# Layer 0 of a four-layer state-space kernel: one shared projection for two scan directions, and two convolution taps per hop instead of three

## The chip, the cores and the metric

The kernel runs on one core of one Trainium2 chip, all in float32. The metric is the time of one execution in microseconds (us), as the device reports it. The core's engines are called by the profile's names: PE (matrix products; PEld is its weight load), DVE (the vector engine), ACT (the scalar engine with its function tables), POOL (GpSimd) and SP, which only issues transfers (SPq, and ACTq for those that ACT issues).

## The reference

Four layers, each with a residual, work on an image batch `x` of shape 2 x 96 x 96 x 96. Each of them runs a selective state-space scan over sequences in four directions. Only layer 0 is changed. Cut to what matters, it is

```python
xin, z = split(in_proj(group_norm(x)))            # 192 channels each
t = gelu(batch_norm(conv3x3(xin, off1_w) + off1_b))
offset = tanh(conv1x1(t, off2_w)) * small         # two numbers per pixel
x_s = bilinear_sample(xin, grid + offset)
xt = x_s cut into 6x6 windows                     # L = 36
xs4 = [rows, columns, rows reversed, columns reversed]
x_dbl = einsum('bkdl,kcd->bkcl', xs4, x_proj_weight)   # k = 4 directions
dts, Bs, Cs = x_dbl[:6], x_dbl[6:22], x_dbl[22:38]
delta = softplus(dt_projs_weight @ dts + bias)
h[l] = h[l-1] * exp(delta[l] * A) + delta[l] * x[l] * B[l];  y[l] = h[l] . C[l]
out = x + out_proj(layer_norm(sum of the four y) * silu(z))
```

Directions 0 and 2 read the same sequence (rows), forwards and backwards; directions 1 and 3 read the columns. So `x_proj_weight` of 0 and 2 is applied to the same numbers, and that of 1 and 3 too.

## The kernel before

**Machine and hops.** A `Machine` object plays one scan over a list of jobs (`Machine.scan`, L449). A job is one direction over one piece of sequence; it has eight steps, called hops, one for each pair of a quarter of the 16 states and a half of the 192 channels. All engines' instructions are written out hop by hop in Python and are kept in that order on each engine. Every buffer is a ring, so an engine that is late holds up the others when their rings are full. Layer 0 has its own machine with T = 288 columns (E = 0); layers 1 to 3 (the trunk) share one with T = 384 (E = 1).

**What a hop issues, in order.** `four_C` (a transfer that spreads four rows of C over 128 partitions) and `four_B` (one matrix product with the 0/1 matrix `sel` that spreads four rows of B, written `pb<-p,sel`), both only in every second hop; transfers that spread delta and delta*x; `sum_states` of two hops earlier (three products `py<-hC,zs`); `decay` of the next hop (three ACT exponentials `dA<-d`); then what was put off to the `slot` of this hop: copies and activations on ACT whose inputs PE made in the hop before; then DVE's four instructions (two products `pd<-w,pb`, two scans `hs<-dA,pd`); `finish` of an earlier job (DVE, reads `py`); the preambles of coming jobs; the background generators (`hop`, L612); and POOL's `hC<-hs,C`. The rings of `hs` and `hC` hold three hops, `dA` two for each sense of direction, `pb` two.

**Layer 0's jobs.** The image is cut into 32 strips of six rows. A strip is eight jobs, 64 hops: two pairs of directions, (0, 2) on rows and (1, 3) on columns, each over two half strips of 288 columns, two directions each. The second job of each two `joins` the first one: both sum into the same `py`. This document writes "hop 7.3" for hop 3 of job 7 of a strip (both counted from 0).

**Preamble** (L362), ten hops ahead of its job (`lead` = 10): in the hop whose number in the eight is 7, two products `pm<-xr,w_wx` (or `xc`) give 80 rows: 6 for dt, 16 for B from row 32, 16 for C from row 64. In the next slot ACT copies them to `j.p` and issues the transfer of the C rows to memory. Then two products `pm<-p,w_dtw` (hops 0 and 1), two ACT evictions `v<-pm,w_scol` (slots 1 and 2), the softplus in slot 2 between two loads of function tables, the transfer of delta, and POOL's `du<-v,xr`. PE has one bank, `pm`, for all of this; `banks = (7, 0, 1)` keeps those hops for the preamble, and the background work takes `pm` in hops 2 to 6 (`bank`, L310).

**Background work of a strip.** `samples` (L824) makes the next strip: affine of the input, then the offsets' convolution (the loop over `tap`), four groups (`po<-x,w_offs`) of nine products of 96 x 96 x 288, each into the one bank `po`; three taps to a hop, then the eviction `t<-po` on ACT in the next slot; then the GELU (with two table loads), the 1x1 convolution `pm<-t,w_off` with tanh, the halving, seven bilinear steps on POOL, the input projection `pm<-top,w_in` and two copies of each piece. `ending` (L735) finishes the last strip: mean and variance (`pm<-yn,mats`, `pm<-sq,mats`), the affine, the gate z (`pm<-xn,w_in`, SiLU), the output projection (`pm<-yn,w_out`). Both run side by side and take turns at `pm`.

## Time and profile before

| | us |
|---|---|
| median of 3 runs | 25900.6 (25885.88 to 25911.11) |
| the profiled execution | 26051.65, its span 26049.9 |
| layer 0, first scan to end of the last (in the profile) | 136.4 to 6863.7 |
| trunk, first scan to last | 7191.5 to 26024.5 |

The time outside the span is 1.75 us. A hop with nothing late lasts 2.92 us, which is DVE's own four instructions. The table below has the mean time of each job of a strip, from the start of its first scan to that of the next job's, over strips 2 to 30 of the profiled execution; it is read from the timeline, two scans to a hop. "Other DVE work" is what DVE does besides its four instructions a hop; "idle" is DVE's.

| job | time | other DVE work | idle | where the idle time lies |
|---|---|---|---|---|
| 0 | 34.06 | 2.78 | 7.95 | hop 1: 3.60, hop 2: 0.49, hop 3: 1.43, hop 4: 1.48, hop 6: 0.95 |
| 1 | 24.90 | 0 | 1.41 | hop 3: 1.22 |
| 2 | 25.09 | 0.98 | 0.73 | hop 3: 0.58 |
| 3 | 27.27 | 0 | 3.67 | hop 2: 1.06, hop 3: 2.40 |
| 4 | 25.54 | 0.98 | 1.20 | hop 1: 0.36, hop 3: 0.72 |
| 5 | 25.06 | 1.76 | 0.08 | |
| 6 | 24.50 | 1.30 | 0 | |
| 7 | 24.64 | 0 | 1.12 | hop 3: 0.59, hop 7: 0.53 |
| strip | 211.05 | 7.8 | 16.1 | |

The convolution's stretch, hop 7.3 to the start of hop 1.0, takes 49.9 us in the mean, and between 41.6 and 65.1 us; whole strips take 201.0 to 228.0 us. The granted PE clock is either full or half in this record, and changes at multiples of 3.41 us.

### The profile page before, as it was taken

Reading aid. Unit: us, or ns where it says so; the run is one execution under the profiler, and the core shown is the slowest. Engines: PE = TensorE matmul, PEld = TensorE weight load, DVE = VectorE, ACT = ScalarE, POOL = GpSimd, SP = SyncE. Lnnn points to the kernel's source line nnn. Section 1 sums busy time; section 2 is a strip of 40 time slices with the busy share of each in tenths; the row PEclk is TensorE's granted clock in tenths of the full one; section 3 lists DMA queues with packets and bytes.
Section 4 is the critical chain, followed back from the end, with each engine's and each line's share of the span. In section 5 each row is a group of like instructions: output and inputs, shape, how many; then the busy total and the mean of one; then the engine's idle time right before and its main releaser. Section 6 shows DMA issues by size and latency. Waiting matters only on the chain.

```text
span 26049.9 us, 281866 instructions
## 1 busy us (share of the span) xinstructions
PE 20979.3 (81%) x70044; PEld 6516.9 (25%) x70044; DVE 24561.8 (94%) x28451; ACT 18515.7 (71%) x40207; POOL 18448.3 (71%) x9188
## 2 busy tenths in 40 slices
PE   7888888888677788888887887778877887877778
PEld 2222222222222222222222222222222222211112
DVE  7989999999589999988999999999999999999999
ACT  5666666666678777777777776677766777666666
POOL 6777777777477777766776666676667766776677
PEclk6655655655577777788877765557755677655566
DMA  3333333333455555555555554555555555544444
GB/s 106 112 107 111 114 110 111 113 112 110 86 150 149 151 158 174 154 149 154 167 172 152 160 154 147 156 166 163 151 153 163 160 161 153 154 148 146 145 145 147
DMA packets 3307209, 3707.97 MB, mean 142 GB/s; under 512 B 781136, under 2 KB 3284822, under 8 KB 3305464
## 3 DMA queue, kind: packets, MB, share of 16 engines
q1 hardware_dynamic: 2587480, 3207.89, 41.0%
q10 hardware_dynamic: 718080, 482.05, 7.7%
q8 instruction: 552, 9.04, 0.1%
q14 instruction: 1097, 8.99, 0.1%
HBM read 2933.11 MB, written 755.57 MB: 142 GB/s over the span
## 4 chain that ended last, share of the span: by engine, by line
DVE 29%; ACT 11%; issue 11%; PE 8%; DMA 3%; POOL 1%; SPq 1%; ACTq 0%; DVEq 0%; POOLq 0%
DVE hs L157 18%; DVE pd L157 10%; PE pm L157 5%; ACT dA L157 5%; ACT L157 2%; PE py L157 2%; SPq L157 1%; PE pb L157 1%; ACT v L157 1%; DVE y L157 1%; POOL hC L157 1%; DMA C<-p 1%; ACT big L157 1%; DMA z<-sz 0%; ACTq L157 0%
## 5 line engine op out<-in xcount | busy, mean ns | idle before, releaser
L157 POOL TENSOR_TENSOR hC<-hs,C 128x1152 f32<-128x1152 f32 (+1 forms) x6656 | 15592.1, 2344 | 7016.7 <-DVE hs L157 4681.1
L157 DVE TENSOR_TENSOR_SCAN hs<-dA,pd 128x772 f32<-128x772 f32 (+2 forms) x13312 | 16047.1, 1245 | 383.7 <-ACT dA L157 241.0
L157 ACT ACTIVATE dA<-d,w_alog 128x384 f32<-128x384 f32 (+1 forms) x19968 | 10281.2, 579 | 4028.9 <-DVE hs L157 3798.1
L157 PE MATMUL py<-hC,zs 128*32 128x384 f32 (+1 forms) x39936 | 7749.6, 676 | 2177.2 <-POOL hC L157 1867.4
L157 DVE TENSOR_TENSOR pd<-w,pb 128x772 f32<-128x772 f32 (+2 forms) x13312 | 8746.4, 701 | 528.3 <-PE pb L157 212.1
L157 PE MATMUL pb<-p,sel 16*128 16x386 f32 (+1 forms) x6656 | 4173.0, 719 | 486.1 <-ACT turn L157 199.1
L157 ACT ACT_TABLE_LOAD x2466 | 3163.9, 1283 | 138.5 <-ACT v L157 92.4
L157 PEld LDWEIGHTS py<-hC,zs 128*32 128x32 f32 x39936 | 1233.4, 129 | 7302.6 <-POOL hC L157 4329.6
L157 PE MATMUL pm<-p,w_dtw 6*96 6x384 f32 (+1 forms) x3328 | 2112.9, 729 | 1106.8 <-ACT v L157 583.2
L157 PEld LDWEIGHTS pb<-p,sel 16*128 16x128 f32 x6656 | 1369.3, 255 | 2528.9 <-DVE hs L157 859.5
L157 PE MATMUL pm<-x,w_taps 96*96 96x384 f32 x3456 | 1591.5, 607 | 192.9 <-ACT v L157 121.7
L157 PE MATMUL pm<-x,w_in 128*96 128x384 f32 (+1 forms) x2448 | 1282.7, 675 | 166.3 <-ACT v L157 75.1
L157 PE MATMUL pm<-xs,w_wx 96*80 96x384 f32 x2304 | 1360.5, 734 | 68.2 <-ACT xs L157 41.1
L157 ACT COPY w<-hc 128x6 f32<-128x6 f32 x4416 | 861.9, 195 | 750.8 <-DVE pd L157 368.9
L157 PEld LDWEIGHTS pm<-p,w_dtw 6*96 6x96 f32 x3328 | 559.8, 219 | 2640.0 <-ACT v L157 1309.0
L157 ACT ACTIVATE v<-pm,w_scol 96x384 f32<-96x384 f32 (+1 forms) x1664 | 909.0, 546 | 214.0 <-issue 100.5
L157 POOL TENSOR_TENSOR du<-v,xs 96x768 f32<-96x768 f32 x576 | 1043.8, 1812 | 7.7 <-ACT v L157 7.6
L157 PE MATMUL po<-x,w_offs 96*96 96x288 f32 x2304 | 885.5, 536 | 49.0 <-ACT x L157 43.0
L157 PEld LDWEIGHTS pm<-x,w_taps 96*96 96x96 f32 x3456 | 632.9, 199 | 1135.7 <-issue 730.9
L157 ACT COPY hc<-hs 128x3 f32<-128x3 f32 x4608 | 827.4, 180 | 4.3 <-DVE hs L157 4.3
L157 PE MATMUL py<-xs,diag 96*96 96x384 f32 x1152 | 654.4, 658 | 151.9 <-ACT y L157 151.9
L157 PEld LDWEIGHTS pm<-x,w_in 128*96 128x96 f32 (+1 forms) x2448 | 503.1, 225 | 980.3 <-issue 448.1
(225 smaller groups left out, 12276.6 us busy)
## 6 DMA issues: line engine op xcount, KB each, us to landing
d<-delta SPq DMA_DIRECT2D x3456, 192.0 KB, 3.7
w<-du SPq DMA_DIRECT2D x3456, 192.0 KB, 3.3
C<-C SPq DMA_DIRECT2D x2304, 192.0 KB, 3.6
d<-delta SPq DMA_DIRECT2D x1536, 144.0 KB, 2.6
w<-du SPq DMA_DIRECT2D x1536, 144.0 KB, 2.6
delta<-v ACTq DMA_DIRECT2D x576, 288.0 KB, 2.6
du<-du SPq DMA_DIRECT2D x576, 288.0 KB, 4.1
C<-C SPq DMA_DIRECT2D x1024, 144.0 KB, 2.8
```

Source lines behind the costliest of these rows:

```text
L157: r = traced(*args, **kwargs)
```

## The change

1. **One projection for two directions** (layer 0 alone). The weights of both directions that read the same sequence are packed into one matrix of 96 rows: dt of the one in rows 0 to 5 and of the other in 6 to 11, B in 32 to 47 and 48 to 63, C in 64 to 79 and 80 to 95. The joining job makes no products `pm<-xr,w_wx`, no copy to `p` and no transfer of C; it uses its partner's `p` and `C`. `p` alternates per two jobs. `w_dtw` has 12 rows, with zeros at the other direction's six; B is spread by a matrix `w_sel` of 32 rows with zeros at the other direction's sixteen; `four_C` of the joining job reads from row 16 on.
2. **Two taps per hop.** The convolution's generator yields after taps 1, 3, 5 and 7 instead of 2 and 5: a group takes five hops (2, 2, 2, 2, 1 taps), the four groups 20 hops instead of 12.

The program of the trunk is the same. Counted over the program, 256 of 35624 PE products go (of `w_wx`), 128 ACT copies, 128 of 256 transfers of C (each of the rest has 32 rows instead of 16), and SP loads one weight more (`w_sel`, 64 x 1024 floats). Counts of all else are equal, those of the table loads too.

The order on the engines moves as follows in a strip (products in PE's hop; ACT's work is in slots, POOL's in hops).

| work | before | after |
|---|---|---|
| convolution taps | 7.3 to 0.6 | 7.3 to 1.6 |
| evictions `t<-po` | 7.6, 0.1, 0.4, 0.7 | 0.0, 0.5, 1.2, 1.7 |
| GELU with two table loads | 1.0 | 2.0 |
| `pm<-t,w_off`, tanh | 1.2 to 1.6 | 2.2 to 2.6 |
| bilinear steps (POOL) | 2.0 to 2.6 | 3.0 to 3.6 |
| `pm<-top,w_in`, copies to xr and xc | 3.2 to 3.6 | 4.2 to 4.6 |
| `pm<-sq,mats` (two) | 2.2, 2.5 | 1.2, 1.5 |
| `yn<-yn,rstd` (POOL, two) | 2.4, 2.7 | 1.4, 1.7 |
| `xn<-x,gn` and two `yn<-yn,w_cols` (ACT) | 3.1 | 2.1 |
| `pm<-xn,w_in` and copies z | 3.6 to 4.5 | 2.6 to 3.5 |
| SiLU with two table loads | 4.6 | 3.6 |
| `yn<-yn,z` (POOL, two) | 4.7, 5.0 | 3.7, 4.0 |
| `pm<-xr,w_wx` or `xc` | hop 7 of every job | hop 7 of jobs 0, 2, 4, 6 |
| copy to `p`, transfer of C | slot 0 of every job | slot 0 of jobs 1, 3, 5, 7 |

```diff
+    xp, dtw = q("x_proj_weight"), q("dt_projs_weight")
+    w, dt = np.zeros((2, 96, 192), np.float32), np.zeros((2 * R, 4, 192), np.float32)
+    sel = np.zeros((64, 2, 4, 32, 4), np.float32)
+    for k in range(4):
+        pair, way = k % 2, k // 2
+        for to, at, n in ((R * way, 0, R), (32 + N * way, R, N), (64 + N * way, R + N, N)):
+            w[pair, to : to + n] = xp[k, at : at + n]
+        dt[R * way : R * way + R, k] = dtw[k].T
+    for way, m, n in np.ndindex(2, 4, 4):
+        sel[32 + N * way + 4 * m + n, way, m, :, n] = 1
+    a["L0_wx"], a["L0_dtw"] = np.stack([_lhsT(v) for v in w], 1), dt
+    a["L0_sel"] = sel.reshape(64, 2, 512)
...
+        self.rows = 80 if E else 96
...
-        j.p = self.p[n % 2]
-        self.own()
-        m = self.mm(self.ps(80)[:, :T], [(layer.wx[:, k, h, :], xs[:, h, :]) for h in range(2)])
-        self.act(lambda m=m: nc.scalar.copy(j.p[:, E : E + T], m))
+        if not j.joins:
+            j.p = self.p[n % 2 if E else n // 2 % 2]
+            self.own()
+            m = self.mm(self.ps(self.rows)[:, :T], [(layer.wx[:, layer.wk(k), h, :], xs[:, h, :]) for h in range(2)])
+            self.act(lambda m=m: nc.scalar.copy(j.p[:, E : E + T], m))
+        else:
+            j.p, j.C = self.jobs[n - 1].p, self.jobs[n - 1].C
...
-        j.C = self.dram.tile([N, T], F32, tag=f"C{T}", name="C", bufs=3)
-        if j.gate is None:
-            nc.scalar.dma_start(j.C, j.p[64:80, E : E + T])
+        if not j.joins:
+            j.C = self.dram.tile([self.rows - 64, T], F32, tag=f"C{T}", name="C", bufs=3)
+            if j.gate is None:
+                nc.scalar.dma_start(j.C, j.p[64 : self.rows, E : E + T])
...
-            m = self.mm(self.ps()[:, :T], [(layer.dtw[:, k, 96 * h : 96 * h + 96], j.p[:R, E : E + T])])
+            m = self.mm(self.ps()[:, :T], [(layer.dtw[:, k, 96 * h : 96 * h + 96], j.p[: layer.dtw.shape[0], E : E + T])])
...
-            nc.sync.dma_start(c, j.C[4 * q : 4 * q + 4, :].unsqueeze(0).to_broadcast([32, 4, T]))
+            at = 4 * q + (N if j.joins else 0)
+            nc.sync.dma_start(c, j.C[at : at + 4, :].unsqueeze(0).to_broadcast([32, 4, T]))
...
-            self.mm(b, [(self.const["sel"][32 : 32 + N, 128 * q : 128 * q + 128], j.p[32 : 32 + N, :])])
+            if E:
+                sel, p = self.const["sel"][32 : 32 + N, 128 * q : 128 * q + 128], j.p[32 : 32 + N, :]
+            else:
+                sel, p = j.layer.sel[32:64, int(j.joins), 128 * q : 128 * q + 128], j.p[32:64, :]
+            self.mm(b, [(sel, p)])
...
+    def wk(self, k):
+
+        return k % 2
...
-                    if tap in (2, 5):
+                    if tap % 2:
                         yield
```

More of the change, by code (lines that the diff above doesn't have):

```diff
@@ L413, in persistent @@
         W = T + 2 * E
-        self.p = [self.sb.tile([80, W], F32, tag=f"p{i}", name="p", bufs=1) for i in range(2)]
+        self.p = [self.sb.tile([self.rows, W], F32, tag=f"p{i}", name="p", bufs=1) for i in range(2)]
         if E:
@@ L644, in load_weights @@
         self.dtw, self.scol, self.cols = self.load("dtw"), self.load("scol"), self.load("cols")
-        self.K = self.wx.shape[1]
+        self.K = self.dtw.shape[1]
         alog = self.load("alog")
@@ L659, in load_weights @@
             nc.vector.tensor_add(self.dsum, self.dsum, D[:, 6:8])
+    def wk(self, k):
+        return k
     def col(self, v, h):
@@ L799, in load_weights @@
         nc = self.nc
-        self.off2 = self.load("off2")
+        self.off2, self.sel = self.load("off2"), self.load("sel")
         self.fold()
@@ L810, in load_weights, with wk @@
         nc.vector.tensor_add(b, b, v(2))
+    def wk(self, k):
+        return k % 2
     def fold(self):
```

## The prediction

> **What bounds the kernel now.** First the page: busy time, and the rows of the 40 slices.

> ```profile
> PE 20979.3 (81%) x70044; PEld 6516.9 (25%) x70044; DVE 24561.8 (94%) x28451; ACT 18515.7 (71%) x40207; POOL 18448.3 (71%) x9188
> ...
> DVE  7989999999589999988999999999999999999999
> ...
> PEclk6655655655577777788877765557755677655566
> ```

> DVE is the bound. The change touches layer 0 alone, the first ten slices, and there DVE has gaps (8s and a 7 among the 9s) while PE has about 0.6 of its clock. So what can be won is DVE's idle time there: 16.1 of 211.05 us a strip, 511 us in 32 strips. Next, who ends that idle time (waits of DVE, 1000 to 6000 us):

> ```profile
> DVE hs L157 <- ACT dA L157: 180.5, 152, 2.4
> DVE yn L157 <- PE py L157: 88.4, 24, 6.8
> DVE yn L157 <- PE pm L157: 70.4, 12, 7.2
> DVE pd L157 <- PE pb L157: 26.1, 25, 2.0
> ```

> Half is a late ACT, half a late PE. The PE half lies in the convolution. The sums by window of two whole strips, then of their convolution stretches (window, us, then PE, PEld, DVE, ACT and POOL busy, granted clock):

> ```profile
> 2432.08:2657.45 225.37, 193.27 (x642) 66.91 (x641) 195.14 (x271) 143.71 (x277) 155.44 (x85) 0.56 0.36 105
> 2865.45:3066.75 201.30, 171.50 (x644) 58.86 (x643) 194.53 (x272) 143.67 (x277) 155.69 (x86) 0.62 0.40 116
> ```
> ```profile
> 2440.83:2505.91 65.08, 64.17 (x177) 27.32 (x177) 41.25 (x58) 27.80 (x55) 30.22 (x17) 0.54 0.30 88
> 2874.20:2915.77 41.57, 40.67 (x178) 18.99 (x178) 40.60 (x57) 28.26 (x57) 30.27 (x17) 0.89 0.47 138
> ```

> The same instructions take 41.57 us at a clock of 0.89 and 65.08 us at 0.54; the strips differ by the same 24 us. PE is busy throughout both. The prices, from PE's timeline at half and at full clock:

> ```profile
> 2450.36 1.18 PE L157 MATMUL py<-hC,zs 128*32 128x288 f32 x6
> 2451.47 3.20 PE L157 MATMUL po<-x,w_offs 96*96 96x288 f32 x6
> 2454.59 1.32 PE L157 MATMUL pb<-p,sel 16*128 16x288 f32 x2
> ...
> 2886.29 0.69 PE L157 MATMUL py<-hC,zs 128*32 128x288 f32 x6
> 2886.91 1.70 PE L157 MATMUL po<-x,w_offs 96*96 96x288 f32 x6
> ```

> From start to start, at half clock: py 1.11, three taps 3.12 (1.04 each), pb 1.25 every second hop. A hop with three taps is 1.11 + 3.12 + 0.63 = 4.86 us of PE against DVE's 2.92, at full clock 2.6. So whether DVE waits depends on when the clock comes up. Last, ACT: the two longest waits for it in the strip before, and the table loads (busy, mean ns).

> ```profile
> 2338.74 2.00 DVE L157 TENSOR_TENSOR_SCAN hs<-dA,pd 128x432 f32<-128x432 f32 x2 [1.41 <-ACT dA L157]
> 2344.15 1.05 DVE L157 TENSOR_TENSOR_SCAN hs<-dA,pd 128x432 f32<-128x432 f32 x1 [2.40 <-ACT dA L157]
> ```
> ```profile
> L157 ACT ACT_TABLE_LOAD x476 | 610.7, 1283 | 67.4 <-ACT v L157 62.2
> L157 ACT COPY p<-pm 80x288 f32<-80x288 f32 x190 | 74.1, 390 | 255.4 <-PE pm L157 255.3
> ```

> These are hops 3.1 to 3.3: the softplus with its tables comes straight after three affines.

> **When the clock comes up.** The clock rows change at multiples of 3.41 us. I took each half-clock step of layer 0 (300 to 6700 us: 1507) with what PE ran in it. 114 were followed by full clock; in all 114 PE was busy throughout, with under 0.15 of pb and w_dtw together, and 319 steps met that in all. Back to half it goes after a step with a gap, and after hardly any other. So PE must be backlogged, and the step must fall between two pb. In the convolution the 30 strips show 24 that come up and 6 that don't (65.0 to 65.1 us).

> [...]

> **The change, part by part, per strip.** The places are those of the table in the section on the change.

> *Taps.* In the stretch 7.3 to 1.0 twelve of 36 taps leave (they go to 1.0 to 1.6), and the w_wx of hop 7.7 (2.1 us at half: four records of 0.52). All at half clock the stretch falls from 65.1 to 65.1 - 12 x 1.04 - 2.1 = 50.5; its floor stays 41.6. Before, the mean lies (49.9 - 41.6)/(65.1 - 41.6) = 0.35 of the way from the floor. I keep this share: 41.6 + 0.35 x 8.9 = 44.7, down 5.2. Is the share right? A hop with two taps is 1.11 + 2.08 + 0.63 = 3.82 us at half clock, still over 2.92: PE stays backlogged, at 0.9 us a hop instead of 1.9. Counting how many steps of 3.41 us fit between two pb (length/3.41 - 1), I get 9 over the old convolution and 8.7 over the new. But two taps make gaps once the clock is up (0.62 + 1.04 + 0.34 = 2.0 against 2.92), so it falls back sooner. Bounds: shares 0 and 1.

> *Job 1* gets the twelve taps and both pm<-sq,mats and loses pm<-t,w_off. PE at half clock: 8 x 1.11 + 4 x 1.25 + 4.3 (mats) + 2 x 1.2 (w_dtw) + 12.5 = 33.1, floor DVE's 23.4. At the same share 23.4 + 0.35 x 9.7 = 26.8; the third group's taps wait in hop 1.2 for an eviction that stands behind the softplus, so 27.0, against 24.9. Bounds 23.4 and 33.1.

> *Job 2, ACT.* GELU with tables (1.28 + 1.16 + 1.28) in slot 0, an eviction and three affines (0.48 + 0.86 + 1.61) in slot 1, softplus (0.48 + 1.28 + 0.68 + 0.37 wait + 1.28) in slot 2, with three dA of 1.37: 14.9 us against 3 x 2.92 + 0.98 = 9.7. Job 1 did this before with 13.5 against 8.8 and DVE lost 1.3, so ACT's lead covers 3.4; DVE loses 5.2 - 3.4 = 1.8. Job 2 was 25.1 with 0.7 lost: now 26.3; with off2 late on PE 26.5. Bounds 25.1 (lead covers all) and 29.6 (no lead).

> *Job 3* loses the affines and the xr, xc copies from the softplus's neighbourhood and gets z copies of 0.39. Of 3.67 idle I leave 0.8, as job 2 had: 24.2. Bounds 23.4 and 27.3. *Job 4* gets the copies to xr, xc (1.06 a slot) and loses w_wx and the copy of p: 25.2 instead of 25.5; bounds 24.4 and 27. Seven bilinear steps of 1.4 on POOL no longer meet the two yn<-yn,rstd (nine POOL steps in eight hops before, seven after, then yn<-yn,z two hops later); I give that nothing of its own.

> *Shared projection.* 256 products (282 us of PE at half clock, 154 at full), 128 copies of 0.39 and 128 issues of 0.32 on ACTq. Nothing more is won: in the hops concerned (jobs 2, 4, 6) DVE has no idle time to give, and its four instructions cover them. Without that cover they would be worth up to 2.2 + 0.39 + 0.32 = 2.9 us a pair of jobs. The wider forms cost nothing: a copy of 96 partitions takes 389 to 396 ns in this window, one of 80 takes 390; a PE record takes 0.48 with 96, 128 or 6 rows alike. A joiner's C lies in memory eight hops sooner than before, and no C transfer stands among the sixty longest waits of that window. w_sel: one load more ahead of everything; the nearest row is x<-in_x, 216 KB in 2.9 us; bounds 0 and 2.9, taken 2.

> Sum: 44.7 + 27.0 + 26.5 + 24.2 + 25.2 + 25.1 + 24.5 + 8.8 (job 7 to hop 3) = 206.0 against 211.05, 5.1 less. 31 strips run the convolution inside the scan: 31 x 5.1 = 158, less 2: 156. The profiled execution, 26051.65, would become 25895; it stands 0.6% above the median of the runs, 25900.6, and I take the 156 us off that: 25745.

> **Rivals.** *The clock stays down.* Thinner taps leave a gap or a pb in nearly every step, or the full clock drains the backlog at once and is lost. For: 6 of 30 strips already miss. Against: 3.82 us a hop still backlogs PE. With share 1, stretch and job 1 are 50.5 and 33.1, the strip 217.9, 6.9 more: 26115. It decides from a share of 0.63 on: 199.4 + 18.6 x share = 211.05. At 0.8 it gives 214.3: 26003.

> *ACT takes PE's place.* Jobs 1 and 2 have no lead, since job 1's evictions already wait for a late PE: 29.6 in job 2, 28.5 in job 1, 210.6 in all: within 15 us of now, 25888. For: ACT ends half of the idle time. Against: job 1 kept its lead before.

> *PE is never late.* Share near 0: 41.6, 23.6 and the rest: 199.5, 25545. For: half the backlog per hop, with rings of three hops to take it. Against: job 1's lump of 33.1 us.

> **Chances.** Forecast (25640 to 25840) 0.45, PE never late 0.15, ACT 0.17, clock down 0.23. The likeliest case's time is 25745; cases on both sides of no change hold weight, so the range reaches from 25590 to 25990. All the bounds together would give 197 to 221 us a strip. A difference of 0.2% (52 us) is what this measurement tells from none. ACT's case lies within it; the clock's case near its turning point gives a little to either side. Faster by more: 0.62, within: 0.17, slower by more: 0.21.

> **What would show it.** The stretch from 7.3 to 1.0 near 45 us, with fewer or no waits of `yn` for `py` over 3 us; job 1 slower by 2; the 2.40 wait in job 3 gone; a new wait of hs for dA of some 2 us at hop 2.3. Wrong, if the mean clock of layer 0's strips falls below 0.56 with the stretch over 48 us, if job 2 loses over 4 us, or if the trunk's time moves.

## The result and the profile after

The changed kernel takes 26066.07 us (median of 4 runs, 26047.98 to 26105.49) against 25902.79 for the kernel before beside it (4 runs, 25885.88 to 25911.11): a ratio of 1.0064 (1.0048 to 1.008), so it is slower by 0.64%. The profiled execution took 26064.07, its span 26062.1. The forecast of 25745 has the wrong sign, and the time lies outside its range.

The page of the kernel after, busy time and slices:

```profile
PE 20939.1 (80%) x69532; PEld 6463.4 (25%) x69532; DVE 24578.3 (94%) x28451; ACT 18483.6 (71%) x40079; POOL 18460.3 (71%) x9188
...
DVE  7999999999589999988999999999999999999999
...
PEclk6555555555577777788877765567755677655556
```

PE has 512 records fewer (two to each of the 256 products) and is busy 40 us less; the work is gone as foreseen. But in the first ten slices, layer 0, the clock row has one 6 where it had four, and DVE's row is the same, digit for digit. The waits of DVE there, 1000 to 6000 us:

```profile
DVE hs L170 <- ACT dA L170: 213.4, 230, 3.0
DVE pd L170 <- PE pb L170: 117.0, 92, 3.8
DVE yn L170 <- PE pm L170: 59.9, 27, 4.3
DVE yn L170 <- PE py L170: 0.9, 1, 0.9
```

The wait the prediction wanted gone is gone: `yn` for `py`, 88.4 to 0.9 us. In its place `pd` waits 117.0 for `pb` (before 26.1), and the scans 213.4 for `dA` (180.5). Next, one strip's convolution stretch (7.3 to 1.0), then jobs 1, 2 and 3, by window (us, busy PE, PEld, DVE, ACT, POOL, granted clock, DMA share, GB/s):

```profile
3934.74:3978.10 43.36, 40.27 (x156) 16.35 (x156) 40.63 (x58) 27.71 (x54) 30.24 (x17) 0.75 0.45 133
3978.10:4006.76 28.66, 25.26 (x87) 9.95 (x84) 23.84 (x33) 15.72 (x32) 19.32 (x11) 0.64 0.33 98
4006.76:4035.60 28.84, 21.00 (x74) 7.18 (x71) 24.66 (x35) 22.83 (x41) 17.59 (x10) 0.57 0.33 97
4035.60:4063.68 28.08, 24.76 (x86) 7.33 (x86) 23.83 (x33) 20.87 (x39) 27.04 (x17) 0.50 0.34 99
```

The stretch is short and DVE nearly full in it (40.63 of 43.36). Each of the three jobs behind it leaves DVE 4.2 to 4.8 us idle, with the clock lower from one to the next. In the mean of strips 2 to 30 DVE is idle for 5.2, 3.9 and 3.9 us in them, where it was 1.4, 0.7 and 3.7. Where these gaps are, from the timeline of the same strip:

```profile
4002.36 2.05 PE L170 MATMUL pm<-sq,mats 96*96 96x288 f32 x4
4004.34 0.75 PE L170 MATMUL pb<-p,w_sel 32*128 32x288 f32 x2
...
4004.44 0.50 ACT L170 ACTIVATE rstd<-pm,eps 96x288 f32<-96x288 f32 x1 [7.16 <-PE pm L170]
4005.12 1.13 DVE L170 TENSOR_TENSOR pd<-w,pb 128x432 f32<-128x432 f32 x2 [3.13 <-PE pb L170]
...
4022.97 2.00 DVE L170 TENSOR_TENSOR_SCAN hs<-dA,pd 128x432 f32<-128x432 f32 x2 [2.40 <-ACT dA L170]
...
4051.65 1.05 DVE L170 TENSOR_TENSOR_SCAN hs<-dA,pd 128x432 f32<-128x432 f32 x1 [3.02 <-ACT dA L170]
```

The variance's products `pm<-sq,mats` now stand behind taps in hop 1.5, and `pb` stands behind them: DVE waits 3.13 us. ACT reads `pm` in order for `rstd` and stands still for 7.16 us, so it enters job 2 with no lead; the GELU, the affines and the softplus then cost DVE 2.40 at hop 2.3, and 3.02 follow in job 3. Over strips 2 to 30, in the table's manner of before:

| | before | forecast | after |
|---|---|---|---|
| stretch 7.3 to 1.0 | 50.0 | 44.7 | 44.1 |
| job 1 | 24.9 | 27.0 | 29.0 |
| job 2 | 25.1 | 26.5 | 28.6 |
| job 3 | 27.3 | 24.2 | 27.7 |
| job 4 | 25.5 | 25.2 | 24.3 |
| strip | 211.1 | 206.0 | 212.1 |
| of it at full clock | 42.1 | not given | 33.4 |

The trunk, first scan to the end of the last, is 18833.0 us before and 18824.1 after; all the rest of this is about layer 0.

### The profile page after: what moved, and what is told of

Its sections match the earlier page's. It is cut to its first block, busy times and chain, and to the rows that moved or that the text cites. A ratio compares the mean times of both kernels' runs of the same rounds, so it can differ in the third digit from the quotient of the medians.

```text
span 26062.1 us, 280655 instructions
## 1 busy us (share of the span) xinstructions
PE 20939.1 (80%) x69532; PEld 6463.4 (25%) x69532; DVE 24578.3 (94%) x28451; ACT 18483.6 (71%) x40079; POOL 18460.3 (71%) x9188
## 4 chain that ended last, share of the span: by engine, by line
DVE 27%; issue 10%; ACT 10%; PE 7%; DMA 3%; SPq 1%; POOL 1%; ACTq 0%; DVEq 0%; POOLq 0%
DVE hs L170 17%; DVE pd L170 9%; ACT dA L170 4%; PE pm L170 4%; ACT L170 2%; PE py L170 2%; SPq L170 1%; ACT v L170 1%; PE pb L170 1%; DVE y L170 1%; ACT big L170 1%; POOL hC L170 1%; DMA C<-p 0%; DMA C<-C 0%; DMA z<-sz 0%
## 5 line engine op out<-in xcount | busy, mean ns | idle before, releaser
L170 PE MATMUL pb<-p,sel 16*128 16x386 f32 x4608 | 2957.5, 732 | 455.8 <-ACT turn L170 194.8
L170 ACT ACT_TABLE_LOAD x2466 | 3163.9, 1283 | 128.5 <-ACT v L170 81.7
L170 PEld LDWEIGHTS pb<-p,sel 16*128 16x128 f32 x4608 | 911.9, 245 | 1904.9 <-DVE hs L170 569.3
L170 PE MATMUL pb<-p,w_sel 32*128 32x288 f32 x2048 | 1220.6, 692 | 71.4 <-DVE pd L170 71.4
L170 PEld LDWEIGHTS pm<-p,w_dtw 6*96 6x96 f32 (+1 forms) x3328 | 565.2, 221 | 2674.4 <-ACT v L170 1365.4
L170 PE MATMUL po<-x,w_offs 96*96 96x288 f32 x2304 | 1015.5, 577 | 106.2 <-ACT t L170 60.1
```

What stands on the lines that cost most here:

```text
L170: r = traced(*args, **kwargs)
```

## The experiments

All of them in one table: median (lowest to highest, runs), ratio to the kernel before on the same chip with its 95% interval, and from each profile the mean strip, its stretch, the three jobs behind, and the us per strip at full clock. "Padded" is explained below. A profile shows one execution, and not always a typical one: that of the taps alone is the fastest of its 12 (25884.94), 90 us below their median. The letter is the chip; the kernel before had medians of 26004.93 (35 runs, a), 25938.88 (23, b) and 25906.59 (8, c).

| kernel | chip | us | ratio | strip | stretch | jobs 1, 2, 3 | full clock |
|---|---|---|---|---|---|---|---|
| before again | a | 26023.14 (25901.3 to 26068.38, 10) | 1.0001 (0.9976 to 1.0027) | 207.4 | 45.5 | 25.2, 25.8, 26.9 | 43.8 |
| projection alone | a | 26052.65 (25998.9 to 26089.08, 12) | 1.0029 (1.0011 to 1.0046) | 212.5 | 51.5 | 25.2, 24.8, 28.2 | 31.4 |
| taps alone | a | 25975.44 (25884.94 to 26045.37, 12) | 0.9994 (0.9975 to 1.0013) | 205.7 | 41.3 | 26.8, 28.3, 26.2 | 51.9 |
| after, variance held back | a | 25956.44 (25875.1 to 26037.58, 12) | 0.9993 (0.9973 to 1.0012) | 208.0 | 42.8 | 24.8, 26.8, 26.4 | 32.0 |
| after again | b | 26092.16 (26062.99 to 26122.94, 12) | 1.0047 (1.0029 to 1.0065) | 212.8 | 43.9 | 29.6, 28.8, 27.8 | 32.6 |
| after, old products unread | b | 26004.54 (25973.29 to 26033.51, 12) | 1.001 (0.9994 to 1.0027) | 209.4 | 43.0 | 27.8, 28.9, 26.7 | 46.3 |
| projection alone, padded | b | 25744.88 (25737.01 to 25756.06, 6) | 0.991 (0.9887 to 0.9933) | 201.4 | 41.2 | 24.5, 24.7, 28.2 | 42.8 |
| after, all padded | b | 25724.39 (25667.05 to 25750.28, 6) | 0.99 (0.9875 to 0.9924) | 200.3 | 41.2 | 23.9, 26.2, 25.8 | 78.7 |
| before, padded | c | 25770.09 (25756.73 to 25777.6, 4) | 0.9939 (0.9915 to 0.9962) | 201.9 | 41.5 | 24.7, 26.0, 26.7 | 48.0 |
| before, 64 rows | c | 26706.64 (26699.03 to 26714.24, 2) | 1.03 (1.0263 to 1.0338) | 232.1 | 66.2 | 30.2, 26.3, 26.7 | 10.1 |
| after, padded | c | 25752.91 (25739.78 to 25764.27, 5) | 0.9927 (0.9903 to 0.9952) | 201.4 | 41.2 | 24.3, 27.0, 25.1 | 59.1 |
| rows and order | c | 25660.78 (25633.01 to 25680.94, 4) | 0.9896 (0.9872 to 0.9921) | 198.0 | 41.1 | 23.5, 24.4, 26.5 | 81.5 |

**Both kernels again.** No edit.

> The kernel before, unchanged, to get a second profile of it. Its first profiled execution took 26051.65 us and its runs 25886 to 25911. Theory A and B (below) both explain 163 us between the runs of the two kernels, but the two profiles differ by 12 us only. If this profile is near 25900, layer 0 (first scan to last) should be near 6580 us instead of 6727, and the mean strip near 206.3 instead of 211, with more strips whose clock comes up early; the trunk 18825 to 18835 as before. If the trunk is what differs, layer 0 stays at 6720 to 6730.

> The changed kernel again, since the runs of the kernel before have turned out to spread from 25872 to 26117 us. If the change truly costs 0.6%: a median near 26160, beside a median before of 26005. If the first runs before were a low draw: 26050 to 26080, ratio 1.001 to 1.003.

The kernel before is not one number: 35 runs of it on one chip lie between 25871.75 and 26116.56, with strips of 201 to 228 us in one execution. The four runs of the first comparison were low in that spread, and the profiled execution that the prediction worked from (26051.65, strip 211.05) was high in it; another profile of the same program took 25924.7, with a strip of 207.4. Between these two profiles layer 0 differs (6727.3 and 6618.5 us), the trunk hardly (18833.0 and 18824.2). The 16 runs of the changed kernel in the two comparisons lie between 26047.98 and 26122.94, and it is slower in the second comparison too, by 0.47%, which lies between the two cases set for it.

**Each part alone.** The projection without the taps, from the kernel after:

```diff
-                    if tap % 2:
+                    if tap in (2, 5):
                         yield
```

> The shared projection with three taps per hop as before. Theory A (the taps cost: the variance's products and ACT's waits for them get into the convolution's hops): 25750 to 25880, not slower than before, since 256 products and 128 copies are gone. Theory B (the projection costs: with fewer full-row products PE is less often backlogged and its clock comes up later): 26000 or more, the convolution's stretch in the profile over 50 us.

The taps without the projection, from the kernel before:

```diff
-                    if tap in (2, 5):
+                    if tap % 2:
                         yield
```

> Two taps per hop with the old projection. Theory A: slower than before by at least as much as the whole change, 26070 to 26250; waits of ACT for the variance's product (rstd for pm) of 150 us or more in 1000 to 6000 us. Theory B: 25850 to 25950.

Less work alone costs 0.29%: the stretch stays at 51.5 us and the clock loses a quarter of its time at full (31.4 us a strip against 42.1 and 43.8 in the two profiles of before). The thinner taps alone can't be told from no change, and their median lies outside the ranges of both theories. In their profile jobs 1 to 3 do take longer, 81.3 us against 77.3 before, but the stretch is at its floor (41.3 us); that is the fast execution named above. The two alone sum to 0.23%, the whole change costs 0.47 to 0.64%, which points to a part that only the two together have.

**The order of the variance.** In the kernel after, the second half of `channel_norm` waits until the last tap is issued, so that both `pm<-sq,mats` leave hops 1.2 and 1.5:

```diff
         t = self.s2("t", 1)
+        self.m.tapping = True
         for h in range(2):
...
+        self.m.tapping = False
+
         def gelu():
...
             r = self.m.tmp.tile([96, self.T], F32, tag="rstd", name="rstd", bufs=self.m.depth)
+            while not self.E and self.m.tapping:
+                yield
             yield from self.spare()
```

> The changed kernel, with the second half of the old strip's ending held back until the convolution has issued its last tap: all of the ending that the change had pulled ahead then follows eight hops later than before the change, as the sampling does. Theory A: job 1 falls from 29.0 to about 25.5 us, job 2 from 28.6 to 26, job 3 from 27.7 to 25, job 4 rises from 24.3 to 27: strip 207 instead of 212, time 25900 to 25940. Theory B: no change, 26050 to 26080.

It takes 0.54% off the changed kernel (0.9993 against 1.0047, two chips, each beside its own kernel before) with no more time at full clock (32.0 us a strip). Jobs 1, 2 and 3 sum to 78.0 us instead of 86.2 (after again), and hop 1.7 loses its idle time (3.03 us in the first profile of the kernel after, 0.23 here). The strip is only 4.8 us shorter, since what was held back falls into jobs 5 and 6, which take 3.2 us more; the median ends 16 us over the range of Theory A. Who waits for PE's `pb`, 1000 to 6000 us of this kernel:

```profile
DVE pd L170 <- PE pb L170: 36.9, 35, 3.1
```

Down from 117.0. `rstd` has left the list of ACT's waits, where it stood with 186.6 us in the kernel after. So this part of the loss is one of order: four records of 96 rows put ahead of `pb` in hops in which PE is behind.

**The removed products put back.** In the kernel after, the joining job makes its two products again, and nothing reads them:

```diff
         else:
             j.p, j.C = self.jobs[n - 1].p, self.jobs[n - 1].C
+            self.own()
+            self.mm(self.ps(self.rows)[:, :T], [(layer.wx[:, layer.wk(k), h, :], xs[:, h, :]) for h in range(2)])
```

> The changed kernel, in which the joining job issues its two products with w_wx again, into a bank that nothing reads: 256 products (282 us at half clock) more on PE, no copy, no transfer. Theory B (the projection's cost is the clock: its products have 96 rows and bring the clock up): the time falls to that of two taps alone, 25940 to 26000, and the full-clock share of layer 0 rises from 0.155 to over 0.2. Theory A (collisions; PE work only costs): 26060 to 26150, share unchanged.

With 256 useless products more, the kernel is 88 us faster (26004.54 against 26092.16 on the same chip), and the clock is full for 46.3 us a strip instead of 32.6; that is Theory B, 5 us over its range. So it is the absence of these products that costs, and it costs through the clock. The copies and transfers of C stay out, so the 88 us are not theirs.

**What the clock counts.** The rule used in the prediction (a step of 3.41 us goes up when PE is busy throughout with little `pb` and `w_dtw`) names the two products with few rows: 16 and 6 of 128. I therefore weighted each PE record with its contraction rows: time x rows / 128, summed over the step (0.48 us a record, which is how far apart the two records of a product start at half clock; `py` at a third, since six of its records take 1.11 us where six of the taps take 3.12). Over the half-clock steps of layer 0 in ten profiles (before, after, and the table's chips a and b), and then in the four later ones (chip c):

| rows in use, share of 128 | steps that went up, ten profiles | four later ones |
|---|---|---|
| under 0.71 | 15 of 12440 | 17 of 4812 |
| 0.71 to 0.73 | 123 of 516 | 12 of 174 |
| 0.73 to 0.74 | 76 of 888 | 55 of 194 |
| 0.74 to 0.75 | 392 of 525 | 124 of 140 |
| over 0.75 | 464 of 542 | 348 of 381 |

A step that went up ranks above one that didn't in 97% of all pairs by this measure, in both sets; by PE's plain busy time in 83 and 78%. The count depends a little on where a record's 0.48 us are put. Put up to its end, none of 17699 steps under 0.71 went up in the fourteen profiles and 1485 of 1540 over 0.75; the ranking is then right in 99.8% of pairs, and in 98.1% if a record is also weighted with its output columns. A tap's records start 0.52 us apart at half clock, so a tap of 96 rows is worth 0.48/0.52 x 96/128 = 0.69, just under the edge; one padded to 128 rows 0.92; one of 64 rows 0.46; `py` 0.86; a `pb` of 16 rows 0.10. By these estimates the taps of 96 rows need `py` beside them and no `pb` to get over it. Two kernels test it with the same number of products at the same price. The first pads the convolution's operands with 32 rows of zeros:

```diff
-        self.offs = self.w.tile([96, 9, 192], F32, tag="offs", name="w_offs")
+        self.offs = self.w.tile([128, 9, 192], F32, tag="offs", name="w_offs")
+        nc.gpsimd.memset(self.offs[96:], 0.0)
...
-        self.xps = [self.sb.tile([96, 8, 98], F32, tag=f"x8{i}", name="x8", bufs=1) for i in range(2)]
+        self.xps = [self.sb.tile([128, 8, 98], F32, tag=f"x8{i}", name="x8", bufs=1) for i in range(2)]
         for x in self.xps:
-            nc.gpsimd.memset(x[:, :, 0:98:97], 0.0)
+            nc.gpsimd.memset(x[:96, :, 0:98:97], 0.0)
+            nc.gpsimd.memset(x[96:], 0.0)
```

> The kernel before with the 32 rows of zeros in the convolution and nothing else. If the clock is all that the taps' rows act on: stretch 41 to 42 us, the spread of the runs below 60 us, 25740 to 25810, that is as fast as the shared projection with the same rows (25745), whose removed work then is worth nothing or up to 50 us.

The second leaves out a third of the offsets' convolution, the channels from 64 on:

```diff
-                        p[:, :288], self.offs[:, tap, 96 * h : 96 * h + 96],
-                        x[:, dy + 3 * i : dy + 3 * i + 3, dx : dx + S], start=tap == 0, stop=tap == 8,
+                        p[:, :288], self.offs[:64, tap, 96 * h : 96 * h + 96],
+                        x[:64, dy + 3 * i : dy + 3 * i + 3, dx : dx + S], start=tap == 0, stop=tap == 8,
```

> The kernel before with the convolution over 64 of its 96 input rows: a third of the offsets' convolution is left out, the same number of products of the same width. If matmul time and the clock didn't depend on rows: 25900 to 26100 as before. If the clock goes by rows in use: taps at 64 of 128 rows never lift it, the clock comes up in the convolution only by chance, stretch 60 to 65 us, strip 222 to 226, 26350 to 26500.

The same strip's stretch in each, by window, first with 128 rows, then with 64:

```profile
3549.71:3591.32 41.61, 40.71 (x178) 18.99 (x178) 40.60 (x57) 28.26 (x57) 30.26 (x17) 0.89 0.46 134
```
```profile
4069.52:4135.74 66.22, 65.32 (x165) 26.83 (x166) 41.25 (x58) 26.11 (x51) 30.15 (x17) 0.50 0.30 87
```

PE is busy for 98 to 99% of both. With 64 rows the clock comes up in none of 29 stretches (0.50), and the kernel loses 3%; with rows of zeros added it is full for 32.5 to 36.9 us of each of them, and the kernel gains 0.61%. The padded kernel came as expected; with 64 rows the loss is larger than expected (26706.64 against at most 26500), since job 1, behind the stretch, takes 30.2 us too. That the products themselves cost the same is seen in PE's timelines, of the kernel with 64 rows at half clock and of the one with 128 at full clock:

```profile
4317.80 3.19 PE L157 MATMUL po<-x,w_offs 64*96 64x288 f32 x6
4320.92 1.18 PE L157 MATMUL py<-hC,zs 128*32 128x288 f32 x6
```
```profile
3770.45 1.70 PE L157 MATMUL po<-x,w_offs 128*96 128x288 f32 x6
```

Three taps of 64 rows take 3.19 us, three of 96 took 3.20 at the same clock; three of 128 take 1.70 us at full clock, as three of 96 did. Only the clock differs. The clock's records hold two states, full and half (807 of each in the profile before, 801 in that after), which change at multiples of 3.41 us; PE's busy share does not tell them apart: 65.32 of 66.22 us busy at 0.50 with 64 rows, 40.71 of 41.61 at 0.89 with 128.

**The change with the clock out of the way.** The padding of above in the projection-alone kernel and in the kernel after:

> The shared projection with three taps, and the convolution's operands with 32 rows of zeros more (128 instead of 96): the same products, the same result. In the six traces so far the clock goes up after a 3.41-us step when the rows in use, averaged over the step, reach some 0.73 of 128, and hardly ever below; a step full of taps with 96 rows lies just under it, with 128 rows well above. Theory B: the clock comes up within two steps of the convolution's first tap in every strip, the stretch takes 42 to 44 us instead of 51.5, the time is 25740 to 25830. If rows don't count, nothing changes: 26030 to 26070.

> The changed kernel with 128 rows in the convolution alone. It sets two taps against three (25745) under a clock that comes up at the first tap. If two taps help for themselves: below 25720. If they only move ACT's and PE's work into worse hops: 25780 to 25900, jobs 1 and 2 longer than with three taps (24.5 and 24.7 us).

The projection alone lands in Theory B's range, its stretch below it (41.2 us). One strip's:

```profile
3544.59:3585.74 41.15, 39.09 (x182) 17.99 (x182) 40.53 (x57) 29.87 (x57) 30.28 (x17) 0.95 0.47 140
```

At 0.95 the taps are no limit at three a hop, DVE has 0.6 us idle, and two a hop (25752.91, strip 201.4) give what three give (25744.88, strip 201.4, on another chip). That is neither of the two cases set for two taps: job 2 takes 27.0 us instead of 24.7, and job 3 25.1 instead of 28.2. The projection, which cost 0.29% before, now costs nothing: strips of 201.4 against 201.9 in the padded kernel before. The intervals of the two ratios (0.9887 to 0.9933 and 0.9915 to 0.9962, on two chips) overlap, so whether it gains is open.

**Rows for the small products too.** The kernel after, padded, and `w_sel` and `w_dtw` padded with zero rows, so that `pb` and `pm<-p,w_dtw` read all 96 rows of `p`:

```diff
-    w, dt = np.zeros((2, 96, 192), np.float32), np.zeros((2 * R, 4, 192), np.float32)
-    sel = np.zeros((64, 2, 4, 32, 4), np.float32)
+    w, dt = np.zeros((2, 96, 192), np.float32), np.zeros((96, 4, 192), np.float32)
+    sel = np.zeros((96, 2, 4, 32, 4), np.float32)
...
-                sel, p = j.layer.sel[32:64, int(j.joins), 128 * q : 128 * q + 128], j.p[32:64, :]
+                sel, p = j.layer.sel[:, int(j.joins), 128 * q : 128 * q + 128], j.p
```

> The changed kernel with 128 rows in the convolution and with all 96 rows of p (zeros in the weights) in the products that spread B and in those with w_dtw, which use 32 and 12 rows now. Theory B: PE's clock comes up whenever PE has a backlog, the late products of jobs 0 to 3 go, strip 201 to 204 instead of 212, time 25700 to 25820. Theory A: the waits in jobs 1 to 3 come from the order on ACT and stay for the larger part: strip 207 to 210, 25900 to 26000.

The clock is full for 78.7 us a strip, the most so far, and the strip 1.1 us shorter than with the convolution padded alone. There was little PE wait left to win (`pd` for `pb` 20.0 us in 1000 to 6000 with the convolution padded alone, 10.8 here); its time can't be told from the other padded kernels'.

**Rows and order.** The last one with three taps a hop, and the affines of `ending` moved away from the softplus, from slot 3.1 to 3.4:

```diff
+        if not self.E:
+            yield from self.step(3, 4)
         if sz is None:
...
-                    if tap % 2:
+                    if tap in (2, 5):
                         yield
```

> Shared projection, three taps, 128 rows in the convolution and 96 in the products from p, and the old strip's affines on ACT moved from the hop before the softplus of job 3 to two hops after it. Theory: with the clock up, what is left is ACT's order; job 3 falls from 28.2 to 24.0 us, strip 197 to 198, 25600 to 25660. If the affines only push a later wait: 25700 to 25745.

The strip came as expected, the time 0.8 us over the upper end, job 3 not: 26.5 us instead of 24.0. Three taps and the moved affines were tried together, so what each of them gives stays open. The page, and DVE's longest waits from 1000 to 6000 us:

```profile
PE 20200.6 (79%) x69532; PEld 6413.4 (25%) x69532; DVE 24546.3 (96%) x28451; ACT 18469.1 (72%) x40079; POOL 18460.8 (72%) x9191
...
PEclk7767777766677777778777755567755676655566
```
```profile
DVE hs L170 <- ACT dA L170: 77.3, 77, 2.1
DVE hs L170 <- POOL hC L170: 8.4, 28, 0.3
```

PE is out of DVE's list of long waits, and what is left of ACT's is 77.3 us of 213.4. At 25660.78 us this is the best version, ahead of both kernels; its four runs (up to 25680.94) also lie below all five of the padded kernel after on the same chip (from 25739.78).

## Why the prediction was wrong

**Taps, stretch: right.** 44.7 forecast, 44.1 and 43.9 measured, and the waits of `yn` for `py` went. The share of 0.35 held by luck as much as by reason: the full clock in it fell from 23 to 18 us, and fewer taps made up for it.

**Two steps failed.** The strip took 212.1 us where the sum gave 206.0. One is the part on the shared projection, the other the terms for jobs 1 to 3. With the removed products put back the strip is 3.5 us shorter, with the variance held back 4.8 (212.8 to 209.3 and 208.0). No run has both edits, so whether the two add up is open.

**The first: "Shared projection. ... Nothing more is won."** It was priced at nothing because DVE's own four instructions cover the hops in which the products ran. That covers their time, not what they did for the clock. Alone it costs 0.29%; with the products put back unread 88 us return. The prediction had in hand that a step goes up only with little `pb` and `w_dtw` in it, read from that a need for a backlog and for steps that fit between two `pb`, and never asked what these two have in common: few rows.

**The second: jobs 1 to 3.** The collisions were seen, their size was missed. Forecast 27.0 + 26.5 + 24.2 = 77.7, measured 29.0 + 28.6 + 27.7 = 85.3. The working counted "both mats" as 4.3 us of PE in job 1, but not that `pb` stands behind them in PE's order and `rstd` in ACT's. It then let "ACT's lead" cover 3.4 us of job 2, a lead that ACT loses in that very wait, and took the 2.40 us out of job 3, where 2.7 stayed in the mean (3.02 in the strip shown). With the variance held back the three jobs take 78.0, nearly the forecast's sum. Job 4 came 0.9 better than forecast; the trunk didn't move.

**The rivals.** "ACT takes PE's place" argued that jobs 1 and 2 have no lead because job 1's evictions wait for a late PE: 28.5, 29.6 and 210.6 a strip, where 29.0, 28.6 and 212.1 were measured. It had 0.17 of the chance and came nearest in the strip, in part by luck: it left job 3 its gain, and what held ACT was `rstd` (186.6 us of waits), while its waits for the evictions' `po` fell from 223.4 to 77.4. Its time, 25888, was off by 178. "The clock stays down" set its price in the stretch, which stayed short; still the layer's share of time at full clock fell from 0.19 to 0.155. Of the signs listed as "wrong if", the clock under 0.56 with a stretch over 48 and the trunk didn't come. Job 2 stood at its sign of 4 us: DVE lost 3.9 there in the first profile and 4.2 in the second. Of the signs that were to show the forecast right, the stretch, the waits of `yn` and the new wait at hop 2.3 came; the wait in job 3 was to go and stayed.

**The base.** Of the 321 us between forecast and result, 169 are those of the profiled execution (it was to be 25895 and was 26064). The other 152 are the offset of 0.6% between the profiled execution and the runs shown, which the prediction carried over as if it were a property of the profiler. It lies within the spread of the kernel before (245 us on one chip); the kernel after spreads by 75, and its profiled execution stands 2 us from its median.

**Slips in the working that decide nothing.** DVE's row of the page has no 8 in its first ten slices: those 8s are the trunk's, and layer 0 at 92% busy shows 9s. 16.1 us in 32 strips are 515 us, not 511. Job 3 with 0.8 us idle is 24.4 by its own row (27.27 - 3.67 + 0.8), not 24.2; job 2 with 1.8 lost is 26.2, not 26.3, and 24.4 if the lead covered all, not 25.1. All the bounds as they stand sum to 196 and 226 us, not 197 and 221.

## What to carry to other kernels

Before a product is removed or split, ask what it does for the PE clock, and count that in contraction rows, not in busy time: where PE was the late engine here, products of 96 rows left the clock to what ran beside them (0.54 to 0.89 in the stretch), products of 64 rows left it at half, and rows of zeros added to the convolution's operands took 0.6 to 1.2% off the three kernels to which they alone were added. An operation that moves into hops where an engine is behind is priced by what stands after it in that engine's order (here DVE waited 3.13 us for `pb` and ACT 7.16 us for the input of `rstd`), and a lead that covers one wait is not there for the next (DVE then lost 2.40 us in job 2 and 3.02 in job 3). One profile of a kernel whose runs spread over 0.9% is a draw, not a base: take a second one before a difference of 0.6% is read from it.
